# Layer 3's forward transform in a written-out order, with eight input groups kept in memory, two weight buffers, and other slots in layer 2

## The chip, the cores and the metric

The program runs on one core of one Trainium2 chip. The metric is the device time in microseconds of one execution. The profiler gives one further execution, with every instruction of the engines PE (TensorE), DVE (VectorE), ACT (ScalarE), POOL (GpSimd) and of the DMA queues; PEld is PE's loading of weights.

## The reference

The input x is 4 x 64 x 256 x 256 in float32. Four layers follow each other, each of the form x + f(group norm of x). Layer 0 is a gated depthwise convolution, layer 1 a 3 x 3 convolution, layer 2 a convolution whose taps are chosen by a threshold, and layer 3, which the change is about, a Fourier layer:

```python
def _L3_conv_ref(x, weights1, weights2):
    x_ft = jnp.fft.rfft2(x)
    w1 = jax.lax.complex(weights1[..., 0], weights1[..., 1])
    w2 = jax.lax.complex(weights2[..., 0], weights2[..., 1])
    top = jnp.einsum('bixy,ioxy->boxy', x_ft[:, :, :M1, :M2], w1)
    bot = jnp.einsum('bixy,ioxy->boxy', x_ft[:, :, H - M1:, :M2], w2)
    out_ft = jnp.zeros((B, Co, H, Wf), dtype=x_ft.dtype)
    out_ft = out_ft.at[:, :, :M1, :M2].set(top)
    out_ft = out_ft.at[:, :, H - M1:, :M2].set(bot)
    return jnp.fft.irfft2(out_ft, s=(H, W))
...
x = x + _L3_conv_ref(_gn(x), L3_conv_weights1, L3_conv_weights2)
```

M1 and M2 are 16: of every channel's 256 x 256 spectrum only 32 x 16 modes are used.

## The kernel before

Each layer reads the tensor that the layer before it wrote to device memory. Layers 0 to 2 write their order out by hand: inside `tc.manual_schedule` the instructions of PE, DVE, ACT and SP stay in the order in which the program names them. Everywhere else a scheduler orders them by priority and by when their operands are free. SP's queue carries the loads and POOL's the stores; a queue is worked off in order, so a load that waits for its buffer holds up the loads behind it.

Six large buffers in memory, the slots, are shared by all layers: three tags y0, y1, y2 of two buffers each (`self.slot(k, name)`). A tag's buffers are handed out in turn, each when its last reader is done.

**Layer 1** uses y0 and y1 for its input x1 (L779 loads) and y2 for the two normalized tiles. Each step normalizes (ACT, L256), transforms by sums and differences (DVE, L842), multiplies into m (PE, L852) and fetches one product as s (ACT, L860).

**Layer 2** goes over 32 row blocks of two halves (n, g). Its input x2_n_g is loaded at L967 into y0 or y1; ACT normalizes it into one of three tiles xn, which are slots for the whole layer (L951: one of y1, two of y2); POOL clears their border columns (L954). The constants peri, thr, scl and wc are loaded once the memory of layer 1 is free. The residual r is loaded at L1004, added at L1123 and stored at L1126.

**Layer 3** has three parts.

The forward part goes over the 4 batches and, in each, over 16 groups of 4 channels (c0). A group is one load of 1 MB (L1217) into a slot, and six groups fit. `psa` (L1258) is the transform along the rows' axis: four matmuls, issued as eight instructions, against the constants `eh`. ACT copies the result to `a` (L1263), PE turns it in four transposes (`psat`, L1267), and DVE copies the two halves into `ah` (L1273), which holds a whole batch with the channel outside and the mode inside. When a batch is complete, `psx` (L1286) transforms along the other axis, ACT copies it to `xw` (L1293), `psxt` (L1299) spreads it over partitions, and DVE scales it by the group norm's factor into `xm` (L1309 to L1311, 24 operations, and two small ones at L1314). No order is written out here. Three blocks of weights of 2 MB each are loaded on the way (`load_w`, L1246).

The mode products (`psm`, L1325) go over eight blocks of two modes k0; a block reads all batches of `xm` and one weight block. Five more weight blocks are loaded into three buffers as these come free. ACT and DVE copy the results to `om` (L1331, L1332).

The inverse part goes over the 64 groups again. It starts with the last six groups of batch 3, which are still in the slots. The others are loaded once more (L1217), into slots or into seven further buffers (`p_x2`). `pst`, `psz` and `psy` transform back, DVE adds the result to x in place (L1383), and POOL stores 1 MB (L1384).

Of the kernel before, what the change touches and what calls it, by code (L numbers as in the profile page):

```python
# [10 lines left out]
F32 = mybir.dt.float32  # L11
U32 = mybir.dt.uint32
AF = mybir.ActivationFunctionType
ALU = mybir.AluOpType
# [3 lines left out]
C = 64  # L18
# [100 lines left out]
class _Net:  # L119
# [812 lines left out]
    def _layer2(self, ctx, src, dst):  # L932
        tc, nc, a, B, H, W = self.tc, self.nc, self.a, self.B, self.H, self.W
# [4 lines left out]
        turn = count()  # L938
# [8 lines left out]
        W1 = W + 1  # L947
        halves = [slice(0, C), slice(C, 128)]
        quarters = [slice(k * Q, (k + 1) * Q) for k in range(4)]

        xns = [self.slot(k, f"xn2_{k}_{i}")[:, 0:10] for i, k in enumerate((1, 2, 2))]  # L951
        z = p_z.tile([128, 2, 10, W + 2], F32, name="z")
        for t in xns + [z[:, 0], z[:, 1]]:
            nc.gpsimd.memset(t[:, :, 0 : W + 2 : W1], 0.0)  # L954
        its = [(b, r0) for b in range(B) for r0 in range(0, H, 32)]
        NI = len(its)
        xt, xn, rt, q, masks, sels, po, bst = ({} for _ in range(8))
# [13 lines left out]
        for n, g in ((0, 0), (0, 1), (1, 0)):  # L971
            for s in range(2):
                load(n, g, s)
        ones = cp.tile([128, Q], F32, name="ones")
        nc.vector.memset(ones, 1.0)
        peri, thr, scl = self.load("peri", cp), self.load("thr", cp), self.load("scl", cp)
# [225 lines left out]
    def _layer3(self, ctx, src, dst):  # L1202
# [2 lines left out]
        M = MODES  # L1205
        NH, NW = H // 128, W // 128
        CC, NK = 4, 2
        NX, NY = 6, 7
        turn = count()

        def load(b, c0, name, pool=None):
            if pool is None:
                x = self.slot(next(turn) % 3, name).rearrange("p r w -> p (r w)")[:, 0 : CC * NH * W]
                x = x.rearrange("p (c n w) -> p c n w", c=CC, n=NH)
            else:
                x = pool.tile([128, CC, NH, W], F32, tag="x", name=name)
            nc.sync.dma_start(  # L1217
                x.rearrange("p c n w -> p c (n w)"),
                src[b][c0 : c0 + CC].rearrange("c (p n) w -> p c (n w)", n=NH),
            )  # L1220
            return x

        first = {c0: load(0, c0, f"x3_0_{c0}") for c0 in range(0, NX * CC, CC)}
        cp = pool(ctx, "l3c", 1)
        eh = self.load("c_eh", cp)
# [8 lines left out]
        halves = [slice(0, C), slice(C, 128)]  # L1234

        with ExitStack() as c2:
            p_w = pool(c2, "l3w", 3)
            p_ah, p_a = pool(c2, "l3ah", 1), pool(c2, "l3a", 3)
            ps_a, ps_t = pool(c2, "l3pa", 2, space=PSUM), pool(c2, "l3pt", 2, space=PSUM)
            ps_x, ps_m = pool(c2, "l3px", 1, space=PSUM), pool(c2, "l3pm", 1, space=PSUM)  # L1240
            wts, xs = {}, {}
            self.small = lambda name: ps_m.tile([128, 512], F32, tag="m", name=name)

            def load_w(k0):
                wt = wts[k0] = p_w.tile([128, 2, NK, M * C], F32, tag="w", name=f"wt_{k0}")
                nc.sync.dma_start(wt, a["wf"][:, :, k0 : k0 + NK])  # L1246

            for b in range(B):

                ah = p_ah.tile([128, NW, C, 4 * M], F32, tag="ah", name=f"ah_{b}")  # L1250
                for c0 in range(0, C, CC):
                    x = first.pop(c0, None) if b == 0 else None
                    x = xs[b, c0] = x or load(b, c0, f"x3_{b}_{c0}")
                    for c1 in range(0, CC, 4):
                        ps = ps_a.tile([128, 2, W], F32, tag="a", name=f"psa_{b}_{c0}_{c1}")
                        for n in range(NH):
                            for j in range(2):
                                nc.tensor.matmul(  # L1258
                                    ps[halves[j]], eh[:, n, :], x[:, c1 + 2 * j : c1 + 2 * j + 2, n, :],
                                    start=(n == 0), stop=(n == NH - 1),  # L1260
                                )
                        m = p_a.tile([128, 2, W], F32, tag="m", name=f"a_{b}_{c0}_{c1}")
                        nc.scalar.copy(m, ps)  # L1263
                        pt = ps_t.tile([128, NW, 2, 2, 4 * M], F32, tag="t", name=f"psat_{b}_{c0}_{c1}")
                        for n in range(NW):
                            for k in range(2):
                                nc.tensor.transpose(  # L1267
                                    pt[:, n, k].rearrange("p j f -> p (j f)"),
                                    m[:, k, n * 128 : (n + 1) * 128], self.ident,
                                )  # L1270
                        c = c0 + c1
                        for n in range(NW):
                            nc.vector.tensor_copy(  # L1273
                                ah[:, n, c : c + 4, :].rearrange("p (j k) f -> p k j f", j=2), pt[:, n]
                            )
                    if c0 % 16 == 0:
                        self.next_norms()
                if b < 3:
                    load_w(b * NK)

                psx = ps_x.tile([128, 4, 128], F32, tag="x", name=f"psx_{b}")
                ahv = ah.rearrange("p n c (s g k r) -> p n g r k s c", s=2, g=4, k=4)
                for n in range(NW):
                    for ri in range(2):
                        for g in range(4):
                            nc.tensor.matmul(  # L1286
                                psx[32 * g : 32 * g + 32].rearrange("p k (s c) -> p k s c", s=2),
                                ew[:, n, ri, :], ahv[:, n, g, ri],
                                start=(n == 0 and ri == 0), stop=(n == NW - 1 and ri == 1),
                                tile_position=(0, 32 * g),  # L1290
                            )
                xw = p_a.tile([128, 4, 128], F32, tag="m", name=f"xw_{b}")
                nc.scalar.copy(xw, psx)  # L1293

                pxt = ps_x.tile([128, 2, 4, 4, 2, M], F32, tag="xt", name=f"psxt_{b}")
                for s in range(2):
                    for k in range(4):
                        for h in halves:
                            nc.tensor.matmul(  # L1299
                                pxt[h, s, k].rearrange("p g r w -> p (g r w)"), xw[:, k, s * C : (s + 1) * C],  # L1300
                                self.ident, start=True, stop=True,
                            )
                r, nb = self.r[3][:, b : b + 1], self.nb[3][:, b : b + 1]
                up, low = halves
                for s in range(2):
                    xb = xm[:, s, :, :, :, b].rearrange("p (g k) w r -> p k g w r", g=4)
                    for k in range(4):
                        v = pxt[:, s, k].rearrange("p g r w -> p g w r")
                        nc.vector.tensor_scalar(xb[up, k], v[up], r[up], None, ALU.mult)  # L1309
                        nc.vector.tensor_scalar(xb[low, k, :, :, 0], v[low, :, :, 1], r[low], -1.0, ALU.mult, ALU.mult)  # L1310
                        nc.vector.tensor_scalar(xb[low, k, :, :, 1], v[low, :, :, 0], r[low], None, ALU.mult)  # L1311
                for k, h in enumerate(halves):
                    dc = xm[h, 0, 0, 0, k, b : b + 1]
                    nc.vector.scalar_tensor_tensor(dc, nb[h], float(H * W), dc, ALU.mult, ALU.add)  # L1314

            for k0 in range(0, M, NK):
                if k0 + 2 * NK < M and k0 > 0:
                    load_w(k0 + 2 * NK)
                wt = wts[k0]
                ps = ps_a.tile([128, 2, W], F32, tag="a", name=f"psm_{k0}").rearrange("p k w -> p (k w)")  # L1320
                ps = ps[:, 0 : NK * M * 2 * B].rearrange("p (k w r b) -> p k w r b", k=NK, w=M, r=2)
                for k in range(NK):
                    for kw in range(M):
                        for s in range(2):
                            nc.tensor.matmul(  # L1325
                                ps[halves[s], k, kw].rearrange("p r b -> p (r b)"),
                                wt[:, s, k, kw * C : (kw + 1) * C],
                                xm[:, s, k0 + k, kw].rearrange("p r b -> p (r b)"), start=True, stop=True,
                            )
                for k in range(NK):  # L1330
                    nc.scalar.copy(om[:, :, :, 0:2, k0 + k], ps[:, k].rearrange("p w r b -> p w b r"))  # L1331
                    nc.vector.tensor_scalar(om[:, :, :, 2, k0 + k], ps[:, k, :, 0, :], -1.0, None, ALU.mult)  # L1332
# [84 lines left out]
```

## Time and profile before

| | us |
|---|---|
| median of 3 runs | 7476.2 (7473.46 to 7483.11) |
| profiled execution, its own time | 7472.07 |
| its span | 7469.9 |
| layer 3, forward part, from the first transposes | 6842 to 7085 |
| layer 3, mode products | 7093 to 7148 |
| layer 3, inverse part | 7148 to 7470 |

The page of the profile gives each engine's busy time, the waits by instruction and releaser, and groups of instructions by source line, with the mean duration. Times inside an execution count from the start of its span. The granted clock is TensorE's, as a part of full speed. The DMA share is the mean busy share of the core's 16 DMA engines; it can pass 1 slightly where packets overlap.

### The profile page before, as it was taken

How to read it: one execution, taken by the hardware profiler on the slowest of the kernel's cores; microseconds unless marked ns; L12 is line 12 of the kernel's file. 1: busy time of each engine (PE TensorE's matmuls, PEld its weight loads, DVE VectorE, ACT ScalarE, POOL GpSimd, SP SyncE). 2: the span in 40 equal slices, each digit the busy share in tenths (PEclk: the TensorE clock that was granted, in tenths of full speed). 3: DMA queues.
4: the chain of work that ended last, by engine and by line, in shares of the span. 5: the costliest groups of instructions: out<-in, count | busy, mean ns of one | idle time of the engine just before them, and what ended most of it. 6: DMA issues, size and time to landing. Idle time of an engine off the chain costs nothing. (4 is left out here: it accounts for less than half of the span.)

```text
span 7469.9 us, 396764 instructions
## 1 busy us (share of the span) xinstructions
PE 7164.3 (96%) x188280; PEld 4283.8 (57%) x188280; DVE 6440.8 (86%) x5705; ACT 3917.9 (52%) x4173; POOL 658.6 (9%) x1435
## 2 busy tenths in 40 slices
PE   6999999999999999999999999899989999998797
PEld 4666666666666666666666666533334444443275
DVE  7999999999999999999999999889979889885345
ACT  3444444444554444454445445377768877773111
POOL 0000000000000000000000000011102222221011
PEclk9999999999999999999999999999999999999955
DMA  3222222222222222222111111399967666667689
GB/s 131 63 64 63 62 63 61 59 63 62 60 62 60 60 63 63 60 61 57 46 46 47 47 46 48 76 223 228 229 149 181 172 178 175 172 173 235 239 350 393
DMA packets 651193, 875.49 MB, mean 117 GB/s; under 512 B 44020, under 2 KB 470212, under 8 KB 647524
## 3 DMA queue, kind: packets, MB, share of 16 engines
q1 hardware_dynamic: 568548, 581.61, 29.0%
q0 software_dynamic: 81024, 268.50, 12.4%
q8 instruction: 1477, 24.20, 1.4%
q14 instruction: 144, 1.18, 0.1%
HBM read 581.50 MB, written 268.44 MB: 114 GB/s over the span
## 5 line engine op out<-in xcount | busy, mean ns | idle before, releaser
L482 PE MATMUL psd<-y,diag 32*32 32x512 f32 x73296 | 2526.3, 597 | 8.0 <-issue 7.6
L520 DVE SCALAR_TENSOR_TENSOR v<-y,sb_w_dw,v 128x2048 f32<-128x2048 f32 x1024 | 2391.5, 2335 | 112.3 <-ACT v L518 89.3
L482 PEld LDWEIGHTS psd<-y,diag 32*32 32x32 f32 x73296 | 1534.6, 103 | 837.3 <-issue 309.9
L462 ACT COPY y<-psy 128x512 f32<-128x512 f32 x1536 | 916.8, 661 | 1671.0 <-PE psy L455 1669.6
L420 DVE TENSOR_TENSOR up<-psu,flt 128x768 f32<-128x768 f32 x1024 | 933.0, 952 | 210.0 <-PE psu L417 209.5
L455 PEld LDWEIGHTS psy<-sb_c_bdft,up 64*64 64x64 f32 x49152 | 855.2, 135 | 340.4 <-issue 127.0
L455 PE MATMUL psy<-sb_c_bdft,up 64*64 64x64 f32 x49152 | 925.0, 221 | 22.8 <-issue 19.5
L417 PE MATMUL psu<-win,xf 64*64 64x384 f32 x8192 | 788.5, 489 | 23.3 <-DVE h L502 10.5
L1038 DVE TENSOR_TENSOR q<-xn 128x2313 f32<-128x2313 f32 (+2 forms) x256 | 628.0, 2496 | 1.7 <-ACT xn L256 1.7
L1093 PE MATMUL one<-z,wp 32*32 32x512 f32 x16384 | 594.6, 597 | 17.6 <-issue 13.1
L1039 ACT ACTIVATE q<-q 128x2313 f32<-128x2313 f32 (+2 forms) x256 | 529.1, 2086 | 32.2 <-DVE q L1038 30.9
L496 ACT ACTIVATE h<-psd 128x1024 f32<-128x1024 f32 x258 | 250.6, 1023 | 516.4 <-PE psd L482 516.4
L256 ACT ACTIVATE xn<-x,nb,r 128x1024 f32<-128x1024 f32 (+3 forms) x272 | 487.1, 1794 | 28.3 <-DMA x<-x 24.4
L1093 PEld LDWEIGHTS one<-z,wp 32*32 32x32 f32 x16384 | 366.9, 103 | 226.4 <-issue 84.6
L1052 PE MATMUL div<-q,ones 64*32 64x512 f32 x8192 | 468.6, 598 | 13.7 <-ACT q L1039 9.8
L427 POOL MEMSET y<- 128x22 f32 x384 | 51.8, 136 | 4212.2 <-ACT y L435 3204.1
L417 PEld LDWEIGHTS psu<-win,xf 64*64 64x64 f32 x8192 | 302.3, 135 | 193.1 <-issue 88.7
L1126 POOL DMA_DIRECT2D x<-r x512 | 273.5, 541 | 971.4 <-DVE r L1123 880.9
L852 PE MATMUL m<-t,wk 64*64 64x512 f32 x3072 | 341.1, 588 | 0.0
L1052 PEld LDWEIGHTS div<-q,ones 64*32 64x32 f32 x8192 | 154.1, 107 | 321.8 <-issue 257.8
L535 DVE TENSOR_TENSOR v<-g,v 64x1024 f32<-64x1024 f32 x257 | 313.5, 1220 | 9.3 <-ACT g L528 1.4
L502 DVE TENSOR_TENSOR h<-h,psd 128x1024 f32<-128x1024 f32 x258 | 302.7, 1215 | 6.1 <-PE psd L482 5.7
(154 smaller groups left out, 7403.2 us busy)
## 6 DMA issues: line engine op xcount, KB each, us to landing
x<-x SPq DMA_DIRECT2D x240, 640.0 KB, 6.6
x<-x SPq DMA_DIRECT2D x122, 1024.0 KB, 10.5
x<-in_x_dram SPq DMA_DIRECT2D x256, 256.0 KB, 3.7
x<-o POOLq DMA_DIRECT2D x128, 512.0 KB, 8.0
r<-x SPq DMA_DIRECT2D x512, 128.0 KB, 4.0
x<-r POOLq DMA_DIRECT2D x512, 128.0 KB, 3.8
out_dram<-x POOLq DMA_DIRECT2D x64, 1024.0 KB, 10.0
r<-in_x_dram SPq DMA_DIRECT2D x248, 256.0 KB, 3.8
```

Of the source, the lines that this page charges most:

```text
L256: self.nc.scalar.activation(dst, src, AF.Identity, bias=self.nb[n][p0:p1, b : b + 1], scale=self.r[n][p0:p1, b : b + 1])
L417: nc.tensor.matmul(ps[halves[n], s, 0:384], xf[t][halves[s], n, 4 * g + k], win[halves[s]], start=True, stop=True)
L420: nc.vector.tensor_mul(ups[t, g][:, :, k, :], ps[:, :, 0:384], flt.broadcast_to([128, 2, 384]))
L455: nc.tensor.matmul(ps[halves[c], n, s, :, k, :], up[halves[n], s, k, i * 128 + c * C : i * 128 + (c + 1) * C], bdft[halves[n]], start=True ...
L462: nc.scalar.copy(yt[t][i][:, 3:11, w0 : w0 + 64].rearrange("p r (k n w) -> p n r k w", k=4, n=2), ps[:, :, s])
L482: ins = nc.tensor.matmul(d[q // 2][quarters[j], q % 2], diag[quarters[q], i, k, :], rows_in(t, i, quarters[q], j, dy)[:, :, dx : dx + W], ...
L520: nc.vector.scalar_tensor_tensor(v, s, wdw[:, 2, k : k + 1], v, ALU.mult, ALU.add)
L852: nc.tensor.matmul(rows2(m)[halves[j], s], w[dx][halves[s]], ts[n][halves[s], i, 2 * j : 2 * j + 2, dx : dx + W], start=(dx == 0), stop=(d ...
L1038: nc.vector.tensor_sub(d, p0, p1)
L1039: nc.scalar.activation(d, d, AF.Square)
L1052: ins = nc.tensor.matmul(ps[quarters[j], h], ones[halves[h]], q[n, g, k][halves[h], r + 2 * j : r + 2 * j + 2, o : o + W], start=(m == 0), ...
L1093: ins = nc.tensor.matmul(rows2(ps[g])[quarters[j], k], w[quarters[i]], z[quarters[i], h, 2 * j + dy : 2 * j + dy + 2, dx : dx + W], tile_p ...
```

## The change

1. Layer 2 makes its three tiles xn after its first loads, from tags 2, 2, 1 instead of 1, 2, 2, and clears borders then.
2. Layer 3 keeps eight groups for six: two more buffers of 1 MB in a pool of their own (`l3k`), taken in turn after the six slots. For that the weights have two buffers for three, and the inverse part five buffers of its own for seven.
3. The forward part's order on PE, DVE, ACT and SP is written out: group i's product and copy, then group i-1's transposes and its copy into `ah`. At a batch's end `along_w` and `spread` stand around the transposes of the next batch's first group. The next group norm's steps are called after `turned`.
4. `ah` has the mode outside and the channel inside.
5. `spread` writes `pxt` so that `xm` is made in six operations for 24.
6. Two weight blocks are loaded in the forward part, after batches 1 and 2, for three; each later one goes out one block of modes ahead, not two.

```diff
-        xns = [self.slot(k, f"xn2_{k}_{i}")[:, 0:10] for i, k in enumerate((1, 2, 2))]
         z = p_z.tile([128, 2, 10, W + 2], F32, name="z")
-        for t in xns + [z[:, 0], z[:, 1]]:
-            nc.gpsimd.memset(t[:, :, 0 : W + 2 : W1], 0.0)
...
         for n, g in ((0, 0), (0, 1), (1, 0)):
             for s in range(2):
                 load(n, g, s)
+        xns = [self.slot(k, f"xn2_{i}")[:, 0:10] for i, k in enumerate((2, 2, 1))]
+        for t in xns + [z[:, 0], z[:, 1]]:
+            nc.gpsimd.memset(t[:, :, 0 : W + 2 : W1], 0.0)
...
-        NX, NY = 6, 7
+        NX, NY = 8, 5
...
-                x = self.slot(next(turn) % 3, name).rearrange("p r w -> p (r w)")[:, 0 : CC * NH * W]
+                k = next(turn) % NX
+                if k < 6:
+                    x = self.slot(k % 3, name).rearrange("p r w -> p (r w)")[:, 0 : CC * NH * W]
+                    x = x.rearrange("p (c n w) -> p c n w", c=CC, n=NH)
+                else:
+                    x = p_k.tile([128, CC, NH, W], F32, tag="k", name=name)
...
+        p_k = pool(ctx, "l3k", NX - 6)
         first = {c0: load(0, c0, f"x3_0_{c0}") for c0 in range(0, NX * CC, CC)}
...
-            p_w = pool(c2, "l3w", 3)
+            p_w = pool(c2, "l3w", 2)
...
+            def turned(b, c0):
+                if c0 == 0:
+                    ahs[b] = p_ah.tile([128, NW, 4 * M, C], F32, tag="ah", name=f"ah_{b}")
...
+                for n in range(NW):
+                    nc.vector.tensor_copy(
+                        ahs[b][:, n, :, c0 : c0 + 4].rearrange("p f (j k) -> p k j f", j=2), pt[:, n]
+                    )
+                if c0 % 16 == 0:
+                    self.next_norms()
...
                 for s in range(2):
-                    xb = xm[:, s, :, :, :, b].rearrange("p (g k) w r -> p k g w r", g=4)
-                    for k in range(4):
-                        v = pxt[:, s, k].rearrange("p g r w -> p g w r")
...
+                    xb = xm[:, s, :, :, :, b]
+                    v = pxt[:, s].rearrange("p g k (r w) -> p (g k) w r", r=2)
+                    nc.vector.tensor_scalar(xb[up], v[up], r[up], None, ALU.mult)
+                    nc.vector.tensor_scalar(xb[low, :, :, 0], v[low, :, :, 1], r[low], -1.0, ALU.mult, ALU.mult)
+                    nc.vector.tensor_scalar(xb[low, :, :, 1], v[low, :, :, 0], r[low], None, ALU.mult)
...
+            with tc.manual_schedule(
+                engines={
+                    mybir.EngineType.PE, mybir.EngineType.DVE, mybir.EngineType.Activation, mybir.EngineType.SP
+                }
+            ):
+                for i in range(len(groups) + 2):
+                    if i < len(groups):
+                        along_h(*groups[i])
+                    b, k = divmod(i - 1, NG)
+                    if b > 0 and k == 0:
+                        along_w(b - 1)
+                    if 0 < i <= len(groups):
+                        turned(*groups[i - 1])
+                    if b > 0 and k == 0:
+                        spread(b - 1)
+                    if i % NG == NG - 1 and i // NG in (1, 2):
+                        load_w((i // NG - 1) * NK)
 
             for k0 in range(0, M, NK):
-                if k0 + 2 * NK < M and k0 > 0:
-                    load_w(k0 + 2 * NK)
+                if k0 + NK < M and k0 > 0:
+                    load_w(k0 + NK)
```

`along_h` holds the load, `psa` and ACT's copy; `along_w` holds `psx` and `xw`; `spread` holds `psxt` and `xm`.

More of the change, by code (lines that the diff above doesn't have):

```diff
@@ L1212, in load @@
             if pool is None:
-                x = self.slot(next(turn) % 3, name).rearrange("p r w -> p (r w)")[:, 0 : CC * NH * W]
-                x = x.rearrange("p (c n w) -> p c n w", c=CC, n=NH)
+                k = next(turn) % NX
[4 more added lines that the diff above has]
+                    x = p_k.tile([128, CC, NH, W], F32, tag="k", name=name)
             else:
@@ L1246, in load_w @@
                 nc.sync.dma_start(wt, a["wf"][:, :, k0 : k0 + NK])
[L1248 to L1279, printed above, removed]
@@ new lines, in _layer3, with along_h @@
+            NG = C // CC
+            ahs, ms, xws = {}, {}, {}
+            ah_of = lambda b: ahs[b].rearrange("p n (s g k r) c -> p n g r k s c", s=2, g=4, k=4)
+            def along_h(b, c0):
+                x = first.pop(c0, None) if b == 0 else None
+                x = xs[b, c0] = x or load(b, c0, f"x3_{b}_{c0}")
+                ps = ps_a.tile([128, 2, W], F32, tag="a", name=f"psa_{b}_{c0}")
+                for n in range(NH):
+                    for j in range(2):
+                        nc.tensor.matmul(
+                            ps[halves[j]], eh[:, n, :], x[:, 2 * j : 2 * j + 2, n, :],
+                            start=(n == 0), stop=(n == NH - 1),
+                        )
+                m = ms[b, c0] = p_a.tile([128, 2, W], F32, tag="m", name=f"a_{b}_{c0}")
+                nc.scalar.copy(m, ps)
@@ new lines, in turned @@
+            def turned(b, c0):
+                if c0 == 0:
+                    ahs[b] = p_ah.tile([128, NW, 4 * M, C], F32, tag="ah", name=f"ah_{b}")
+                m = ms.pop((b, c0))
+                pt = ps_t.tile([128, NW, 2, 2, 4 * M], F32, tag="t", name=f"psat_{b}_{c0}")
+                for n in range(NW):
+                    for k in range(2):
+                        nc.tensor.transpose(
+                            pt[:, n, k].rearrange("p j f -> p (j f)"), m[:, k, n * 128 : (n + 1) * 128], self.ident
+                        )
+                for n in range(NW):
+                    nc.vector.tensor_copy(
+                        ahs[b][:, n, :, c0 : c0 + 4].rearrange("p f (j k) -> p k j f", j=2), pt[:, n]
+                    )
+                if c0 % 16 == 0:
+                    self.next_norms()
@@ L1281, in _layer3, with along_w @@
+            def along_w(b):
                 psx = ps_x.tile([128, 4, 128], F32, tag="x", name=f"psx_{b}")
-                ahv = ah.rearrange("p n c (s g k r) -> p n g r k s c", s=2, g=4, k=4)
                 for n in range(NW):
@@ L1287, in _layer3 @@
                                 psx[32 * g : 32 * g + 32].rearrange("p k (s c) -> p k s c", s=2),
-                                ew[:, n, ri, :], ahv[:, n, g, ri],
+                                ew[:, n, ri, :], ah_of(b)[:, n, g, ri],
                                 start=(n == 0 and ri == 0), stop=(n == NW - 1 and ri == 1),
@@ L1291, in _layer3, with spread @@
                             )
-                xw = p_a.tile([128, 4, 128], F32, tag="m", name=f"xw_{b}")
+                xw = xws[b] = p_a.tile([128, 4, 128], F32, tag="m", name=f"xw_{b}")
                 nc.scalar.copy(xw, psx)
-                pxt = ps_x.tile([128, 2, 4, 4, 2, M], F32, tag="xt", name=f"psxt_{b}")
+            def spread(b):
+                xw = xws.pop(b)
+                pxt = ps_x.tile([128, 2, 4, 4, 2 * M], F32, tag="xt", name=f"psxt_{b}")
                 for s in range(2):
@@ L1299, in _layer3 @@
                             nc.tensor.matmul(
-                                pxt[h, s, k].rearrange("p g r w -> p (g r w)"), xw[:, k, s * C : (s + 1) * C],
-                                self.ident, start=True, stop=True,
+                                pxt[h, s, :, k], xw[:, k, s * C : (s + 1) * C], self.ident, start=True, stop=True
                             )
@@ L1305, in _layer3 @@
                 for s in range(2):
-                    xb = xm[:, s, :, :, :, b].rearrange("p (g k) w r -> p k g w r", g=4)
-                    for k in range(4):
-                        v = pxt[:, s, k].rearrange("p g r w -> p g w r")
-                        nc.vector.tensor_scalar(xb[up, k], v[up], r[up], None, ALU.mult)
-                        nc.vector.tensor_scalar(xb[low, k, :, :, 0], v[low, :, :, 1], r[low], -1.0, ALU.mult, ALU.mult)
-                        nc.vector.tensor_scalar(xb[low, k, :, :, 1], v[low, :, :, 0], r[low], None, ALU.mult)
+                    xb = xm[:, s, :, :, :, b]
[3 more added lines that the diff above has]
+                    nc.vector.tensor_scalar(xb[low, :, :, 1], v[low, :, :, 0], r[low], None, ALU.mult)
                 for k, h in enumerate(halves):
@@ L1314, in _layer3 @@
                     nc.vector.scalar_tensor_tensor(dc, nb[h], float(H * W), dc, ALU.mult, ALU.add)
+            groups = [(b, c0) for b in range(B) for c0 in range(0, C, CC)]
+            with tc.manual_schedule(
[15 more added lines that the diff above has]
+                        load_w((i // NG - 1) * NK)
             for k0 in range(0, M, NK):
-                if k0 + 2 * NK < M and k0 > 0:
-                    load_w(k0 + 2 * NK)
+                if k0 + NK < M and k0 > 0:
+                    load_w(k0 + NK)
                 wt = wts[k0]
```

## The prediction

> **What bounds the kernel now.** I read the page's engine rows first, then stages by the table of windows, then the waits of layer 3's forward part, then single instructions there, and last the border between layers 1 and 2, since the change touches layer 2's slots.
>
> ```profile
> PE 7164.3 (96%) x188280; PEld 4283.8 (57%) x188280; DVE 6440.8 (86%) x5705; ACT 3917.9 (52%) x4173; POOL 658.6 (9%) x1435
> 5500.00:5510.00 10.00, 0.49 (x8) 0.00 (x0) 0.00 (x0) 3.51 (x3) 0.00 (x0) 0.63 0.56 115
> 6842.00:7085.00 243.00, 197.41 (x1008) 70.33 (x1008) 73.20 (x208) 39.25 (x68) 0.00 (x0) 0.99 0.74 263
> 7085.00:7093.00 8.00, 0.00 (x0) 0.00 (x0) 7.63 (x25) 0.00 (x0) 0.00 (x0) 0.80 0.00 0
> 7093.00:7148.00 55.00, 54.79 (x1024) 54.73 (x1024) 3.73 (x14) 5.40 (x15) 0.00 (x0) 0.50 0.50 193
> 7148.00:7470.00 322.00, 266.03 (x1408) 204.07 (x1408) 180.12 (x290) 39.31 (x66) 48.22 (x64) 0.56 1.01 398
> ```
>
> After the stretch and its length, a window row has the busy time of PE, PEld, DVE, ACT and POOL, then granted clock, DMA share and GB/s. The whole span is PE's, but the edit's stages are not. In the forward part (6842 to 7085) PE is busy for only 197 of 243 us and DMA for 0.74. The inverse part (7148 on) is DMA's: share 1.01. At 5500 PE stands still for nearly 10 us.
>
> ```profile
> ACT a L1263 <- PE psa L1258: 166.8, 62, 5.1
> PE psat L1267 <- ACT a L1263: 42.9, 57, 1.8
> DVE xm L1309 <- PE psxt L1299: 39.1, 4, 10.0
> ACT xn L256 <- DMA x<-x: 16.1, 1, 16.1
> PE m L852 <- ACT s L860: 9.6, 1, 9.6
> ```
>
> Each wait row has total, times and longest. PE and ACT alternate: PE stops 57 times for ACT's copy of the group just multiplied. The last two rows belong to 5490 to 5510: ACT sits 16.1 us on one layer 2 load, and PE behind it 9.6 us.
>
> ```profile
> 6907.49 4.59 PE L1258 MATMUL psa<-x,sb_c_eh 128*64 128x512 f32 x20
> 6912.02 1.09 PE L1267 MATMUL psat<-sb_c_ident,a 128*128 128x128 f32 x8
> 6918.67 1.93 PE L1258 MATMUL psa<-x,sb_c_eh 128*64 128x512 f32 x6
> 6921.33 0.66 PE L1267 MATMUL psat<-sb_c_ident,a 128*128 128x128 f32 x4 [0.73 <-ACT a L1263]
> L1286 PE MATMUL psx<-ah,ew x128: 1024/1035/1043, 6892.3 to 7080.7; 128*32 128x512 f32 x128
> L1332 DVE TENSOR_SCALAR om<-psm x16: 265/266/268, 7100.5 to 7149.0; 128x64 f32<-128x64 f32 x16
> ```
>
> The first two rows are a stretch without that wait: 0.226 us per product instruction, 0.136 per transpose. The next two are the usual rhythm, with 0.73 us idle; psat starts 6921.33 and 6924.59 give 3.25 us per group. The four psx starts lie some 60 us apart: 16 groups at 3.25 and about 8 of border.
>
> **The change, part by part.** Sums are against the profiled execution (span 7469.9, its own time 7472.07); the median 7476.2 stands 4.1 above it.
>
> *1. Fixed order.* The next group's eight product instructions go ahead of a group's four transposes, so ACT's copy (0.59) runs under 8 x 0.226 = 1.81 us of PE. A group costs PE 1.81 + 4 x 0.136 = 2.36. Two products are done before 6842, where the first copy is released by layer 2's last stores (that wait stays). So 64 x 2.36 - 2 x 1.81 = 147 us.
>
> *2. The other layout of ah* (mode outside, channel inside). psx now reads channels 256 B apart: 1035 ns, against 592 for psa's contiguous 512. Before, 32 psx instructions take 6.98 us; at psa's rate, four column groups at once instead of two, 32 x 0.453 / 4 = 3.6. psxt stays 1.75, with about 0.6 for ACT's copy between them, which the next group's transposes partly cover: four borders, 4 x 5.95 = 24. Forward PE: 147 + 24 = 171 us, against 242.3 before (6842.2 to the end of the last psxt, 7084.45).
> The price is on DVE: its copies into ah (416 ns for 256) now write 256 B apart. The nearest row is L1332, strided writes out of PSUM: 266 ns for 64. With 149 ns fixed from the ah copy (416 - 256 x 1.04), it took 1.83 ns an element; so 149 + 256 x 1.83 = 617 ns. [...] were the copies slowed by psx's factor (1035/592), 416 would become 728. Two copies then make 1.23 to 1.46 us a group, under PE's 2.36: hidden beside PE, except before the last psx, +0.5. Lower bound 416 (no loss); the upper is the second rival's.
>
> *3. DMA's supply.* After 6842 the forward part must still fetch about 54 groups of 1.049 MB and two weight blocks of 2.097 MB: 61 MB. The rate when the queue is full is in these rows (GB/s last):
>
> ```profile
> 6840.00:6845.00 5.00, 3.17 (x14) 2.15 (x15) 1.74 (x6) 1.07 (x2) 0.00 (x0) 0.56 1.07 417
> 6995.00:7000.00 5.00, 4.26 (x21) 1.38 (x20) 1.51 (x4) 0.58 (x1) 0.00 (x0) 1.00 1.03 399
> 7000.00:7005.00 5.00, 3.52 (x20) 1.52 (x20) 0.87 (x3) 1.17 (x2) 0.00 (x0) 1.00 1.02 393
> ```
>
> [...] At the rows' 395 it is 154 + 15 = 169, just under PE. I take the rows, since they are reads of this very stage, and add 3 us for waits at so close a race. Forward part: 242 to 174, -68. The eight groups in memory instead of six are what lets DMA run on through a border, where it stops today (share 0.00 at 6895 to 6900).
>
> *4. Constants behind loads.* On SP the two new buffers' loads stand before eh's, which psa needs. They reuse layer 2's memory and go out when its last matmul ends, 6826.7, as eh does now. eh then lands behind 2.1 MB, about 5 us later; psa(0) goes from 6830 to about 6835 and two cold products (5.35) end near 6840.5. ACT's copy is held till 6841.6 by the stores, so 0; without that cover, 5.
>
> *5. Fewer, larger xm writes.* Per batch 24 small operations (8 x 440, 16 x about 338 ns) become six. From L1309 against L1310, 100 ns for 64 more elements: 240 + 1.56 ns each, so 512 take 1.04 us and 256 take 0.64: 4.6 plus the two small ones. Only the last batch's lie on the path (7084.5 to 7093.0, 8.6 us): -3.6. [...]
>
> *6. Weights in two buffers.* In the mode products a block takes 6.83 us (ACT om copies at 7100.10 and 7106.93), and a 2 MB load lands in 7.4 (median of five there). With two buffers a load may start only when the block two before is done, so it has one block to hide under: 7.5 - 6.83 = 0.7, in about every second of six: +2. Bounds: 0, if loads in overlap keep pace, and 6, if each is late by 1. The third early load leaves the forward part: that is in point 3.
>
> *7. Inverse part.* Two loads fewer, 2 x 1.049 MB at 411 GB/s: -5.1. But five loads can be out at once before the first store frees a slot, not seven: 13 us of DMA work where the first store comes 15 us in. I give back 1.5: -3.6.
>
> *8. Layer 2's slots.* The load of x2_0_1 today takes the slot that layer 1 frees last, behind eight r loads on SP. In the changed order on SP it follows x2_0_0 and takes one freed two steps sooner. ACT's normalization of it then waits for DVE's last transform instead. Behind ACT's wait stands its copy s for row block 62, whose buffers PE needs. In the new order only normalize(0,0) stands ahead of that copy: DVE's transform ends 5491.2, two memsets, 2.8 us of ACT, so s starts near 5494.4, well before PE runs dry at 5500.5. PE keeps its 9.6 us [...]. normalize(0,1) ends near 5504, when PE has 7 us of layer 1 left. -10; at worst -4 if ACT's later chain ends last, at best -11. The r loads move behind a later x load; they are first used near 5585, 80 us of cover.
>
> Sum: -68 + 0.5 - 3.6 + 2 - 3.6 - 10 = -82.7, rounded -82. Profiled 7390, median 7394.
>
> **Rivals.**
> *DMA bounds the forward part* [...]: 14 us less, 7408. For it: share 0.9 already at 325 GB/s. Against it: 387 to 434 in every stretch where something queues.
> *DVE becomes the bound, and the kernel slower.* If strided copies cost X, a group takes 2X; past X = 1.18 us DVE leads. All of 82 us and the 15 of the measurement's bound are gone when 64 x (2X - 2.36) = 97, at X = 1.94, 4.7 times today's 416. At X = 2.0 it is 7394 + 64 x 1.64 = 7499. Nothing in the trace has such a factor: 1.75 on PE, under 2 at L1332.
> *The border gain fails* (another wait takes ACT's place; the shift is absorbed at layer 2's start, where constants, not loads, are waited for): 7404.
> *The order does nothing*, since the scheduler already puts one product instruction ahead of the transposes: PE's 43 us of waits stay, 7394 + 43 = 7437. Against it: the new order on PE has all of them ahead.
>
> **How the numbers follow.** Main 0.62; DMA-bound 0.16; border 0.10; order 0.07; DVE 0.03; the remaining 0.02 is no change. The main case with its unknowns (copies, weights, border, 3 us of waits) spans about 7381 to 7404; with the first and third rival together (24 us), and some way to the fourth, the range is 7381 to 7424. 0.2%, about what a measurement of this kernel can tell from no change, is 15 us: faster 0.95, same 0.02, slower 0.03.
>
> **What would show it.** Right: psat starts about 2.4 us apart with no idle on ACT a; psx near 600 ns; ah copies 0.6 us with DVE idle; no 16 us wait of ACT at 5490; waits for wt under 1 us; inverse share still 1.0. Wrong: PE psa waiting for DMA x by more than 10 us in all; DVE the releaser of psat; blocks over 8 us apart.

## The result, and the profile after

The median went from 7478.8 (7473.5 to 7483.1, four runs) to 7400.4 us (7396.6 to 7402.9, four runs): a ratio of 0.9895, interval 0.9878 to 0.9912. That is 78 us less; 82 was predicted. The profiled execution took 7396.64 (span 7394.6) against 7472.07: 75 less. In the comparisons further down two executions, one of the kernel before (7645.7) and one of the changed kernel (7782.4), are left out of the medians, since they were some per cent slower at a lower granted clock (0.923 and 0.872, for 0.97).

The engine row of the page:

```profile
PE 7146.5 (97%) x188280; PEld 4285.9 (58%) x188280; DVE 6443.3 (87%) x5633; ACT 3917.6 (53%) x4173; POOL 658.6 (9%) x1435
```

PE's busy time is 18 us shorter; the rest of the gain is idle time that has gone. Where it went shows in the windows (length, then PE, PEld, DVE, ACT, POOL, granted clock, DMA share, GB/s):

```profile
5500.00:5510.00 10.00, 10.00 (x96) 3.51 (x92) 7.09 (x7) 7.63 (x7) 1.31 (x3) 1.00 1.01 219
6833.00:7013.00 180.00, 176.36 (x1020) 68.86 (x1016) 84.92 (x164) 39.22 (x67) 1.09 (x2) 1.00 0.94 350
7017.00:7075.00 58.00, 54.88 (x1020) 54.68 (x1018) 3.72 (x14) 5.28 (x14) 0.00 (x0) 0.50 0.58 219
7075.00:7395.00 320.00, 270.61 (x1410) 208.87 (x1408) 180.33 (x290) 39.44 (x66) 48.22 (x64) 0.54 1.00 394
```

The hole in layer 1's last steps is gone: PE runs without a break until layer 1 ends at 5516. The next hole, at the start of layer 2, stays: PE waits 10.5 us there for DVE (L1038), where the kernel before waits 10.3 for a load of constants. The forward part is 180 us long and PE is busy for 176 of them. The mode products have the same 55 us of work in 58. The inverse part is as long as it was. The rhythm of the forward part, from the timeline:

```profile
6834.02 1.94 PE L1264 MATMUL psa<-x,sb_c_eh 128*64 128x512 f32 x8
6835.88 0.66 PE L1279 MATMUL psat<-sb_c_ident,a 128*128 128x128 f32 x4
6836.47 1.94 PE L1264 MATMUL psa<-x,sb_c_eh 128*64 128x512 f32 x8
6838.34 0.66 PE L1279 MATMUL psat<-sb_c_ident,a 128*128 128x128 f32 x4
```

Psat starts lie 2.46 us apart (6835.88, 6838.34), and no row carries an idle time in brackets. A border (the end of a batch) adds 5.6 us in all to two groups (psat starts 6.03 and 4.44 apart). The instructions whose addressing changed, and the new xm operation (minimum, median and maximum in ns):

```profile
L1283 DVE COPY ah<-psat x128: 544/602/616, 6834.1 to 7005.0; 128x256 f32<-128x256 f32 x128
L1295 PE MATMUL psx<-ah,ew x128: 592/592/617, 6873.3 to 7008.2; 128*32 128x512 f32 x128
```

```profile
L1319 DVE TENSOR_SCALAR xm<-psxt,r x8: 1105/1140/1147, 6879.7 to 7013.9; 64x512 f32<-64x512 f32 x8
```

What PE still waits for from layer 2's end to the last mode product (total, times, longest):

```profile
PE psa L1264 <- DMA sb_c_eh<-in_c_eh_dram: 11.3, 1, 11.3
PE psm L1356 <- DVE xm L1324: 5.1, 1, 5.1
PE psm L1356 <- DMA wt<-in_wf_dram: 3.1, 3, 1.1
```

No row says psa waits for x.

### The profile page after: what moved, and what is told of

Read it like the earlier page. It is cut to its first block, busy times and chain, and to the rows that moved or that the text cites. A ratio compares the mean times of both kernels' runs of the same rounds, so it can differ in the third digit from the quotient of the medians.

```text
span 7394.6 us, 396690 instructions
## 1 busy us (share of the span) xinstructions
PE 7146.5 (97%) x188280; PEld 4285.9 (58%) x188280; DVE 6443.3 (87%) x5633; ACT 3917.6 (53%) x4173; POOL 658.6 (9%) x1435
## 5 line engine op out<-in xcount | busy, mean ns | idle before, releaser
L1038 DVE TENSOR_TENSOR q<-xn 128x2313 f32<-128x2313 f32 (+2 forms) x256 | 627.8, 2495 | 1.7 <-ACT xn L256 1.7
L1052 PEld LDWEIGHTS div<-q,ones 64*32 64x32 f32 x8192 | 153.5, 107 | 318.3 <-issue 252.8
```

Source lines behind the costliest of these rows:

```text
L1038: nc.vector.tensor_sub(d, p0, p1)
L1052: ins = nc.tensor.matmul(ps[quarters[j], h], ones[halves[h]], q[n, g, k][halves[h], r + 2 * j : r + 2 * j + 2, o : o + W], start=(m == 0), ...
```

## The experiments

All ran on one chip, another than the comparison above. Layer 0 takes 4853 to 4875 us there in the profiles, where it took 4826 and 4831, and layer 2 behind layer 1 varies by up to 15 us between profiles. So the verdicts rest on stages inside the profiles, one profile for each kernel, taken between first and last starts, with the ratio to the kernel before beside them. The kernel before has no profile on this chip; its row is from the first one.

- layer 1: last psd of layer 0 to last m
- start: last `one` of layer 2 to first psat
- forward: first psat to last psxt; xm: from there to first psm
- modes: first to last psm; inverse: from there to the end

| kernel | layer 1 | start | forward | xm | modes | inverse | median | ratio to before (interval) |
|---|---|---|---|---|---|---|---|---|
| before | 695.8 | 16.1 | 242.0 | 8.9 | 54.5 | 322.3 | 7478.8 | |
| after | 684.3 | 18.0 | 177.9 | 5.4 | 58.1 | 319.8 | 7400.4 | 0.9895 (0.9878 to 0.9912) |
| after, other chip | 684.9 | 20.3 | 177.7 | 5.4 | 58.1 | 320.0 | 7441.8 | 0.9896 (0.9881 to 0.9912) |
| 1 slots alone | 686.0 | 16.8 | 241.6 | 8.9 | 54.5 | 320.6 | 7506.0 | 0.9979 (0.9971 to 0.9986) |
| 2 order alone | 697.0 | 16.8 | 212.7 | 8.8 | 54.6 | 320.6 | 7474.4 | 0.9940 (0.9922 to 0.9957) |
| 3 old ah | 684.8 | 17.3 | 191.0 | 5.4 | 57.9 | 318.3 | 7451.4 | 0.9912 (0.9896 to 0.9927) |
| 4 eh first | 684.9 | 15.7 | 180.3 | 5.4 | 57.8 | 320.2 | 7439.5 | 0.9893 (0.9871 to 0.9914) |
| 5 six groups, three weight buffers | 685.3 | 16.1 | 186.9 | 5.4 | 54.5 | 321.0 | 7450.8 | 0.9910 (0.9895 to 0.9925) |
| 6 no order | 685.6 | 19.4 | 229.0 | 5.4 | 57.9 | 318.2 | 7492.7 | 0.9970 (0.9959 to 0.9981) |
| 7 early inverse loads | 685.2 | 15.3 | 177.7 | 5.4 | 58.3 | 319.7 | 7447.5 | 0.9908 (0.9893 to 0.9923) |
| 8 old xm | 684.9 | 17.7 | 191.7 | 8.8 | 58.1 | 320.8 | 7455.6 | 0.9920 (0.9903 to 0.9936) |
| 9 other memory | 684.8 | 9.0 | 177.9 | 5.4 | 57.8 | 320.5 | 7434.3 | 0.9890 (0.9876 to 0.9904) |
| 10 and weights in ah | 683.9 | 8.2 | 177.7 | 5.4 | 54.4 | 320.7 | 7429.7 | 0.9882 (0.9868 to 0.9896) |

The kernel before had 7515.5 to 7521.1 as its median beside these runs. By the ratios alone many of these kernels can't be told from the changed one: their intervals overlap. How well the stages repeat shows in the rows "after" and "after, other chip".

### 1 and 2: one part of the change in the kernel before

Run 1 puts only layer 2's lines into the kernel before:

```diff
-xns = [self.slot(k, ...) for i, k in enumerate((1, 2, 2))]
-for t in xns + [z[:, 0], z[:, 1]]: nc.gpsimd.memset(...)
 ... load(n, g, s)
+xns = [self.slot(k, ...) for i, k in enumerate((2, 2, 1))]
+for t in xns + [z[:, 0], z[:, 1]]: nc.gpsimd.memset(...)
```

> The kernel before with layer 2's slots and border clearing of the changed kernel alone. Theory: the 16 us wait of ACT between layers 1 and 2 goes and PE stops there 10 us less, nothing else moves: profiled span 7460, a median 10 below the kernel before. Rival (the gain is absorbed at layer 2's start, where PE waits for constants): the median of the kernel before, within 3.

Layer 1 to its last m takes 686.0 instead of 695.8, or of 697.0 in run 2, which has the old slots on the same chip: 10 to 11 us. That is PE's wait of 9.6 and a slow restart: the eight products behind it take 1.99 us in the kernel before (granted clock 0.50 from 5509.5 to 5512), where eight usually take 1.04. Forward, modes and inverse stay within 2 us, and layer 2 behind layer 1 does not take the gain back beyond its own spread. The rival falls. By the ratio the gain is 16 (interval 11 to 22).

Run 2 has the written-out order alone (in outline):

```diff
+with tc.manual_schedule(engines={PE, DVE, Activation, SP}):
+    for i in range(len(groups) + 2):
+        along_h(i); along_w at a border; turned(i - 1); spread at a border
```

> The changed kernel's written-out order of the forward part alone: six groups kept, three weight buffers, the old layout of ah, the old 24 operations into xm and layer 2's old slots. Theory (PE sets the forward part once the order hides ACT's copy): a group takes PE 2.45 us instead of 3.25, a border keeps psx at 1035 ns, so 64 x 0.8 = 51 less, of which some 6 go where the first groups wait for layer 2: median 45 below the kernel before, the forward part 197 instead of 242. Rival (with six slots DMA stops at each border and cannot catch up): psa waits for x after each border, and the gain is below 30.

The forward part is 29 us shorter, not 45. The order alone leaves PE other waits (rows of PE):

```profile
PE psat L1274 <- DVE ah L1278: 8.4, 3, 2.8
...
PE psa L1259 <- DMA x<-x: 4.9, 4, 1.8
```

The two rows hold 13 of the 16 us that are missing; slower restarts come on top (3.12 to 3.68 us for eight products, for 1.94; last section). The rival named the second row, yet the first is the larger: DVE's copies into ah stand behind something. Run 8 shows what. By the ratio the gain is 45 (interval 32 to 59), more than the 29 of the stages. But the profiled execution is the longest of this kernel's four, 7493.3, and lies 28 below the median of the kernel before, as the stages have it: a good part of the surplus is the spread between executions. The rest stays open.

### 3: the old layout of ah

```diff
-ahs[b] = p_ah.tile([128, NW, 4 * M, C], ...)
+ahs[b] = p_ah.tile([128, NW, C, 4 * M], ...)
```

> The changed kernel with the channel outside and the mode inside in ah again: psx reads strided, the copies into ah write contiguous. Theory (PE sets the forward part): psx goes from 592 back to 1035 ns an instruction, each of the four borders costs 3.4 us more, the shorter copies give 0.4 back before the last psx: 13 us above the changed kernel. Rival (DMA's supply sets the forward part): three of the four borders only give DMA time to catch up, so 3 us above the changed kernel.

Forward 191.0: 13.3 more, as PE's sum said. The inner borders pay too (psat starts 9.44 apart instead of 6.03). If DMA's supply had set the forward part, three of the four would have been free, as the rival had it.

### 4: the constants ahead of the two new loads

```diff
-first = {c0: load(...) for c0 in range(0, NX * CC, CC)}
+first = {c0: load(...) for c0 in range(0, 6 * CC, CC)}
 eh = self.load("c_eh", cp)
 ...
+for c0 in range(6 * CC, NX * CC, CC): first[c0] = load(...)
```

> The changed kernel with the constants eh and ew loaded ahead of the loads into the two new buffers. Theory as predicted (ACT's copy is held by layer 2's last stores in any case): no change, the first psat stays 17.4 us behind layer 2's last matmul on PE. Rival (the wait for eh is paid, since psa of the second group now stands ahead of the first transposes): eh lands some 5 us sooner, two cold products are done before the stores are, the first psat comes 1.8 us sooner and the time falls by 2 to 4.

Each is right in part. psa waits 3.3 us for eh, where the changed kernel waits 13.4 on this chip, and the first psat comes 15.7 us behind layer 2's last matmul, against 17.3 to 20.3 in the runs with the same memory and eh behind the loads. But the forward part takes 2.6 more, and the ratio shows no gain clear of noise. From the timeline of PE (idle time and its releaser in brackets):

```profile
6844.49 5.35 PE L1266 MATMUL psa<-x,sb_c_eh 128*64 128x512 f32 x16 [3.29 <-DMA sb_c_eh<-in_c_eh_dram]
6856.26 1.12 PE L1281 MATMUL psat<-sb_c_ident,a 128*128 128x128 f32 x4 [6.42 <-ACT a L1271]
6857.31 3.68 PE L1266 MATMUL psa<-x,sb_c_eh 128*64 128x512 f32 x8
```

psa is early, and then PE stands for ACT's copy, which starts only 15 us behind layer 2. The trace does not name layer 2's stores as the cause; run 9, in which `a` and `ah` lie in other memory and this wait is gone, makes them likely. After those 6.42 us eight products take 3.68 instead of 1.94: the clock fell (granted 0.50 from 6855 to 6860). The saved time goes into this restart. The first row above is the two products that the expectation calls cold: 5.35 us for 16 instructions, which take 3.7 in the rhythm.

### 5: the trade of memory undone

```diff
-NX, NY = 8, 5
+NX, NY = 6, 7
-p_w = pool(c2, "l3w", 2)
+p_w = pool(c2, "l3w", 3)
-load_w((i // NG - 1) * NK)    # behind batches 1 and 2
+load_w((i // NG) * NK)        # behind batches 0, 1 and 2
 ...
-load_w(k0 + NK)               # in the mode products
+load_w(k0 + 2 * NK)
```

> The changed kernel with the trade of memory undone: six groups kept, seven further buffers in the inverse part, three weight buffers and a third early block of weights. Theory (supply counts as much as PE: with the eight groups DMA moves at its full rate until just before PE's last group): 2.1 MB more in the forward part and six slots make psa wait for x around the borders, some 10 us, as in the run with the order alone; the mode products get 3.5 us shorter, the inverse part 2 longer: 9 above the changed kernel, forward part 188 instead of 178. Rival (the prediction's account, in which waits for x are worth 3 us): 0 to 2 below the changed kernel, forward part at most 181.

Forward 186.9, 9.2 more, modes 3.6 less. PE's rows:

```profile
PE psat L1274 <- ACT a L1264: 7.4, 2, 7.2
PE psa L1259 <- DMA x<-x: 5.3, 3, 3.8
```

psat starts 7.74 and 3.88 apart, each the last group ahead of a border, are 5.3 and 1.4 over the rhythm; behind the 3.8 us wait eight products also take 3.36 us for 1.94. Another 2 are a slow first group (1.12 us for its four transposes and 3.53 for the eight products behind them, after 7.22 of waiting for ACT's copy), as in run 4, since here eh is not behind two loads. So the theory holds for the forward part. Start and modes give much of it back: layer 3 as a whole is 2 to 5 us longer than in the two profiles of the changed kernel. The median is 9 above the changed kernel's, with intervals that overlap. The trade is worth a few us; how much of that is the eight groups and how much the block of weights less in the forward part is not separated.

### 6: the order undone

```diff
-with tc.manual_schedule(...): ...
+for b, c0 in groups:
+    along_h(b, c0); turned(b, c0)
+    # behind a batch's last group:
+    along_w(b); spread(b)
```

> The changed kernel without the written-out order: a group's products, its transposes and the border's work are named one after the other, and the scheduler orders them. All else stays. Theory (the order hides ACT's copy): a group takes 3.25 us again and the forward part 178 + 64 x 0.8 less the cover that the borders lose, about 228: 45 to 50 above the changed kernel. Rival (the eight groups and the layout carry the gain, the scheduler already runs one product ahead): a group below 2.7 us, at most 20 above.

Forward 229.0, where 228 was expected. The timeline has the old wait back:

```profile
6898.24 0.66 PE L1279 MATMUL psat<-sb_c_ident,a 128*128 128x128 f32 x4 [0.72 <-ACT a L1269]
6898.83 1.94 PE L1264 MATMUL psa<-x,sb_c_eh 128*64 128x512 f32 x8
6901.49 0.66 PE L1279 MATMUL psat<-sb_c_ident,a 128*128 128x128 f32 x4 [0.72 <-ACT a L1269]
```

3.25 us a group; PE waits 62 times for ACT's copy in the forward part, 45 us in all. The rival falls. The order is worth 29 us put in alone (run 2) and 51 taken out last: in run 2, waits for DVE and x take its place.

### 7: inverse loads ahead of time

```diff
+xq = p_ah.tile([128, 4, CC, NH, W], F32, tag="ah", name="xq")
+for j in range(4):
+    into(xq[:, j], *parts[NX + j])
 for k0 in range(0, M, NK):
```

> The changed kernel with four of the inverse part's first groups loaded into the memory of ah as soon as its last reader is done, ahead of the third block of weights; the inverse part then has those four buffers and one more, as many as before. Theory (the inverse part is DMA's, and DMA is idle for 26 us around the start of the mode products): 4.2 MB at about 400 GB/s leave the inverse part: 310 instead of 320, the mode products stay at 58, 10 below the changed kernel. Rival (the loads delay the weights, or the inverse part's start is set by the transposes): mode products 62 or more, inverse part 318, no gain.

The theory falls. Of the rival, the half on the start of the inverse part holds, the half on the weights does not. The loads run when DMA was idle (330 GB/s from 7061 to 7073), the weights are not delayed, and the inverse part still takes 319.7. Its first 20 us, this kernel and then the changed one:

```profile
7127.00:7147.00 20.00, 16.50 (x105) 11.04 (x104) 12.61 (x22) 3.16 (x6) 1.57 (x2) 0.76 0.34 126
```

```profile
7075.00:7095.00 20.00, 17.30 (x102) 11.67 (x100) 11.63 (x19) 3.17 (x6) 1.57 (x2) 0.67 0.90 332
```

4.1 MB less move here (126 against 332 GB/s over 20 us), and DMA stands still instead, at a share of 0.34: two stores start in these 20 us (POOL's x2), and SP takes from 7127.2 to 7180.0 to send out nine loads. That loads wait for stores at this point is seen in the changed kernel:

```profile
SPq L1221 <- DMA out_dram<-x: 56.4, 12, 14.7
```

The row is for 7075 to 7147. In run 7 DMA's share is 1.02 to 1.04 only from 7147 on. Loads taken off the start of this part buy nothing.

### 8: the 24 small operations into xm

```diff
-nc.vector.tensor_scalar(xb[up], v[up], ...)
+for k in range(4):
+    nc.vector.tensor_scalar(xb[up, k], v[up], ...)
 ... and so for the two on low
```

> The changed kernel with the 24 small operations into xm a batch again, and psxt's old layout with them. Theory (in the fixed order these operations stand between two groups' copies into ah on DVE, and PE's transposes wait for those): the third group behind each of the first three borders takes 5.3 instead of 2.45 us, 8.5 in all, and the last batch's operations 3.5: 12 above the changed kernel. Rival (only the last batch's operations lie on the path, as predicted): 3.5 above, no group over 3 us outside the borders.

With them goes the old order of psxt in its buffer. xm is 3.4 longer, as both said, and the forward part 14.0. PE's row, and its timeline behind the first border:

```profile
PE psat L1279 <- DVE ah L1283: 9.2, 3, 3.1
```

```profile
6930.43 0.63 PE L1279 MATMUL psat<-sb_c_ident,a 128*128 128x128 f32 x4 [3.06 <-DVE ah L1283]
6930.98 2.93 PE L1264 MATMUL psa<-x,sb_c_eh 128*64 128x512 f32 x8
6933.85 1.12 PE L1279 MATMUL psat<-sb_c_ident,a 128*128 128x128 f32 x4
```

DVE runs the 24 operations and the two at L1326 from 6920.8 to 6929.3, ahead of the copies into ah; psat has two buffers, so its third group waits 3.06 us. Then PE runs at a lower clock for a while (granted 0.74 from 6930.0 to 6933.8): 2.93 for eight products, 1.12 for four transposes. That makes 4.7 us a border, 14 for three; the theory's 8.5 left the clock out.

### 9 and 10: the start and the weights

Run 4 showed two waits behind each other. Run 9 takes away both: `p_a` is opened first and `p_ah` ahead of `p_w`, so that neither should lie in memory which layer 2's last stores still read, and the constants come ahead of the two loads. (For room, the inverse part's z takes a's buffers.)

```diff
+p_a = pool(ctx, "l3a", 3)
 p_k = pool(ctx, "l3k", NX - 6)
 ...
-p_w = pool(c2, "l3w", 2)
-p_ah, p_a = pool(c2, "l3ah", 1), pool(c2, "l3a", 3)
+p_ah = pool(c2, "l3ah", 1)
+p_w = pool(c2, "l3w", 2)
```

> The changed kernel with another order of layer 3's memory: a and ah lie where layer 2's last stores do not read, and the constants stand ahead of the loads into the two new buffers. (z takes a's buffers in the inverse part, for room.) Theory (two waits stand behind each other at layer 3's start, for eh and for layer 2's stores, and taking one away alone gave nothing; DMA's supply starts when the first psa frees a buffer, so it comes earlier with PE): psa starts 4 us behind layer 2's last matmul instead of 12, the first psat 9 behind it instead of 17.4, and the forward part keeps its 178: 8 below the changed kernel. Rival (DMA bounds the forward part): the first psat comes sooner, but psa waits for x later on, the forward part takes 183 or more, at most 3 below.

Start 9.0, forward 177.9. The timeline of PE:

```profile
6864.38 5.22 PE L1267 MATMUL psa<-x,sb_c_eh 128*64 128x512 f32 x16 [3.30 <-DMA sb_c_eh<-in_c_eh_dram]
6869.54 0.66 PE L1282 MATMUL psat<-sb_c_ident,a 128*128 128x128 f32 x4
```

One short wait is left. DMA holds the pace (377 GB/s at a share of 1.01 from 6870 to 7038) although PE starts 9 to 11 us sooner: psa never waits for x, as the theory said, which has the loads start sooner with the first freed buffer. The median is 7.5 below the changed kernel's, and the intervals of the ratios overlap.

Run 10 adds four weight blocks in ah's memory:

```diff
+wq = p_ah.tile([128, 2, 2, NK, M * C], F32, tag="ah", name="wq")   # blocks 2, 3, 6, 7
+load_w(2 * NK)
+load_w(3 * NK)
 for k0 in range(0, M, NK):
-    if k0 + NK < M and k0 > 0: load_w(k0 + NK)
+    if k0 + 3 * NK < M and k0 > 0: load_w(k0 + 3 * NK)
```

> As the run before, and blocks 2, 3, 6 and 7 of the weights are loaded into ah's memory once its last reader is done, so that the mode products have four buffers. Theory (the 3.1 us of waits for weights in the mode products are the price of two buffers): mode products 54.5 instead of 58, in all 11 to 12 below the changed kernel. Rival (the block is set by something else than the buffers): 58, as in the run before.

Modes 54.4 instead of 57.8: those 3.4 us were the price of two buffers. 7429.7 is 12 below the changed kernel on the same chip and 86 below the kernel before; the intervals of the ratios still overlap (0.9868 to 0.9896, and 0.9881 to 0.9912), but the stages show both gains.

The changed kernel itself, for these comparisons:

> The changed kernel once more, on the same chip as the two runs before, for a comparison on one chip: layers 0 to 2 differ by some 40 us between chips. Forward part 178, mode products 58, inverse part 320; 75 to 82 below the kernel before.

Its stages repeat those of the other chip to 0.2 us in layer 3, but for the start, and to 0.6 in layer 1.

## Why the prediction was right, point by point

Right in direction and size. Nearly all errors lie on one side: forward part, start, weights and inverse part together gave 8.5 us less than forecast, and only layer 2's slots gave more, 1.5. The stages of the profiles before and after sum to -75: layer 1 -11.5, start +1.9, forward -64.1, xm -3.5, modes +3.6, inverse -2.5; layer 0 (+5.8) and the rest of layer 2 (-5.0) vary by as much with no cause in the change.

- *Fixed order, PE's sum.* The mechanism is shown (run 6). The sum of a group was too small: it takes 2.45, not 2.36, since each change between products and transposes adds some 0.05 (1.86 from psa to psat and 0.59 back, for 1.81 and 0.54), +6 over 64 groups. That the 3 us booked for waits did not come is luck: it hides half of this. The forward part gave 64 for 68.
- *Layout.* psx 592 as said, and a border's 32 take 3.64 us for 7.05 (four start within 0.02 us of each other, the next four 0.43 to 0.45 later); ah copies 602 for 617, the estimate by the strided row L1332. The 1.04 ns an element in that estimate is what DVE takes at L571 of the kernel before: 418 ns for 256 elements, 683 for 512. At the one stride tried here, 256 B, PE's reads take 1.75 times as long (1035 for 592) and DVE's writes 1.45 times (602 for 416). Worth 13.3 (run 3), with DVE's longer copies hidden beside PE.
- *Supply.* DMA moved 375 GB/s from 6833 to 7001 at a share of 1.01, and psa never waited for x. The 14 us of the rival in which DMA bounds this part were the author's estimate, and no run shows them. But 375 is below the 395 that the prediction took from its rows: its 61 MB then take 163 us, 178 with the 15 of work that it put behind the last landing, which is what the forward part took. PE, busy for 167.5 of the same 168 us, and DMA were full together, and the reserve is thin: six slots and 2.1 MB more bring the waits back (5.3 us for x, run 5).
- *eh behind the loads.* Predicted 0, measured about 2 (start 18.0 for 16.1; 20.3 for 16.8 on the other chip). psa(0) came 12 us behind layer 2, where the prediction had 8 and the kernel before has 4. The cover was real: with eh early (run 4) ACT's copy still starts 15 us behind layer 2. But in the changed kernel psa(0) ends only then, and psa(1) stands ahead of psat(0) in the new order.
- *xm.* -3.5 for -3.6. What failed is "only the last batch's lie on the path": true of the kernel before, where PE's transposes wait only 1.2 us in all for DVE's copies. In the new order the 24 operations would have cost another 14 (run 8). The forecast never missed it, since it summed PE alone for a kernel in which they are gone.
- *Weights.* +3.6 for +2, in the bounds of 0 and 6 (runs 5 and 10): three waits of about 1 us, for three of 0.7.
- *Inverse.* -2.5 for -3.6, and hardly out of the spread: kernels with eight groups give 318.2 to 320.8, with six 320.6 to 322.3. The step that failed took bytes at the start of a stage with a DMA share of 1.00 for time (run 7).
- *Layer 2's slots.* -11.5 for -10; alone 10 to 11 (run 1). In the kernel before, SP sent out the load of x2_0_1 at 5494.72, behind eight r loads that took from 5481.46 to 5494.6, 9.0 us of it in waits.

In the forward part order alone 29, layout 13, xm 14 and memory 9 make 65, against 64. That they meet is in part chance: the first is put in alone, the others are taken out of the whole, and with the order taken out (51) the sum would be 87. The parts depend on each other. The prediction booked nearly all of it to the order and the layout.

## What to carry to other kernels

A wait that leaves makes room for the next one (in run 2 the order brought waits of 13.3 us for DVE and x): price a reorder by the sum of the engine that shall lead, then ask for each other queue whether it keeps that pace, because a part that was free before (24 small DVE operations in a border's slack) may be what holds the new order up (14 us in run 8). In a stage like the inverse part, whose DMA share is 1.00, look at the first microseconds: loads wait for stores there (56.4 us in the changed kernel), and 4.1 MB less at that point gave nothing (319.7 for 320.0 us, run 7). Which memory a new stage's first tiles lie in may decide what they wait for (the 6.42 us of run 4 are gone in run 9); of two waits behind each other, the one taken away alone gave nothing here (run 4), both together 9 to 11 us (run 9).

## What had not been expected of the hardware

A stall of PE can cost more than its length. In run 8 an idle time of 3.06 us, and in run 4 one of 6.42, was followed by slower products (2.93 and 3.68 us for eight, against 1.94). The window behind the first:

```profile
6930.00:6933.80 3.80, 3.37 (x12) 1.01 (x12) 2.14 (x5) 0.00 (x0) 0.00 (x0) 0.74 0.91 326
```

The granted clock is 0.74 there and 1.00 in the 5 us before, so 3.06 us became 4.7 a border. The length of a stall does not decide this alone. From the timeline of PE in run 2:

```profile
7043.61 3.47 PE L1259 MATMUL psa<-x,sb_c_eh 128*64 128x512 f32 x8 [1.80 <-DMA x<-x]
7068.77 0.63 PE L1274 MATMUL psat<-sb_c_ident,a 128*128 128x128 f32 x4 [2.80 <-DVE ah L1278]
7069.33 1.94 PE L1259 MATMUL psa<-x,sb_c_eh 128*64 128x512 f32 x8
```

After 1.80 us of idle time eight products take 3.47, while after 2.80 they take 1.94. Two other stalls of 2.80 in that run were followed by 3.12 and 3.63, and one of 1.85 by 1.94. What decides between them stays open. After waits of 0.7 us eight products still took 1.94 us (run 6); in the kernel before, with the same waits, the granted clock was 1.00 from 6850 to 7050. A PE that is busy by this profile does not ensure a clock of 1.00 either: in the mode products PE is busy for 55 of 58 us at a granted clock of 0.50, and no run asks why.
